# A two-layer graph transformer kernel: the widest block of destination nodes is worked in two halves, and the first table pieces start four steps later

## The chip, the cores and the metric

The kernel runs on one core of a Trainium2 chip. The metric is the time on the device for one execution, in microseconds. The core's engines are TensorE (PE), VectorE (DVE), ScalarE (ACT), GpSimd (POOL) and the queue of SyncE (SP); in the profile PEld is PE's weight load.

## The reference, cut to what matters

6250 nodes with 128 values each, 100,000 edges, 16 node types, 32 edge types, 8 heads of 16 values. Two layers like this one, a last linear map, a residual and a layer norm:

```python
k, q, v = (typed_linear(x, ntype, W).reshape(n, H, HS) for W in (Wk, Wq, Wv))
kT = jnp.einsum('nhd,htdo->nhto', k, Watt)      # a K row for every node and edge type
vT = jnp.einsum('nhd,htdo->nhto', v, Wmsg)
a = jnp.einsum('ehd,ehd->eh', kT[src, :, etype], q[dst]) * pri[:, etype].T / SQRT_D
att = edge_softmax(a, dst, n)                   # over the edges of one destination
hag = segment_sum((vT[src, :, etype] * att[:, :, None]).reshape(-1, H * HS), dst)
h = silu(typed_linear(hag, ntype, Wa))
h = layernorm(h * alpha + x * (1 - alpha)) * g + b
```

## The kernel before, in words

A first part sorts the nodes by type class and degree and writes layer 0's table to DRAM: for every node and edge type one row of 256 values, K and V (the table stores of L1110). From about 607 us on the function `edges` does both layers.

**Blocks and slots.** The destination nodes stand in 49 blocks of 128, one node a partition. A block has so many slots: slot j holds the j-th edge of each node. The widths are `OWN` (25, 21, 19, 18, 17, 16, 15, 14, 13, 12, 11) for each of four type classes and `SHARED` (41, 20, 17, 15, 14) for nodes of all classes. A slot costs one gather: POOL issues an indirect DMA (L1722) that brings 128 rows of the table, one a partition, to the ring `kvr` of `SLOTS` = 50 slots in SBUF. Nodes with very many edges take lanes of further slots: of the 41 slots of the widest block the last 12 are "riders". They get no gather; an SP copy (L1715) moves a few rows from a gathered slot (27 or 28) to them. So this block has 29 gathers and 12 copies.

**The order.** Superblocks of two to four blocks are visited in the order of `ORDERS`, one string a layer; layer 0's begins 1c 3c 1a 1b +a 2a. 1c and 3c have 13 + 12 + 11 slots each, 1a has 25 + 21 + 19 + 18 = 83 (one of them a rider), 1b 17 + 16 + 15 + 14. +a is the 41-slot block and one of 20; in layer 1 it follows 1c. POOL's order is the order in which the code is written out (`manual_schedule`); the other engines' instructions are placed by a scheduler from the same code. Layer 1's first two superblocks are begun early, under layer 0.

**One block.** Its gathers go out in chunks of up to 8 slots (`bring`, L1699); a chunk starts where the ring pointer stands and is cut at the ring's end, and if fewer than `CH` = 4 slots are left when a block begins, the pointer goes to 0 (L1668). A gather into a slot waits until DVE has last read the slot. For each chunk DVE multiplies the K half by the node's query (L1738) and sums by head (L1743). `bundles_of` (L1461) gives the order of the 41-slot block: slots 0-7 first, then 21-28 with the twelve riders, whose K products wait until the copies have read slots 27 and 28, and last 8-20.

**The rest of a block.** `finished` (L1503) is a generator. It is advanced one step a slot while the next block's slots are issued (`step`, L1688): mask (L1508), maximum (L1514), difference (L1523), exponential on ACT (L1525), its sum (L1528), then for each chunk the V half times the weights (L1541) and the adding up into the accumulator `acc` of four slots (L1552), and at the end its sum (L1557). The weights stand in the PSUM pair if 256 + 8K columns (layer 0) fit in 512, else in the SBUF tile `a`. With a superblock's last block, the node work `nodes` (L1814) is spread over the coming slots: hag (L1779), typed linear maps (masks of L300, products of L317), activation, layer norm.

**Layer 1's table.** Layer 0's `nodes` ends with K and V of the new nodes (L1895, L1899). `table` (L1599) spreads the generator `pieces_of` (L1938) over the slots of the superblock two visits on. Of each block it makes two tiles: PE products (L341), four ACT copies to the tile `st` (L348; three buffers), and a scatter on POOL (L1944), which is put in the queue 5 half steps after the tile, at the start of the next chunk's gathers (`put_due`, L1717). A superblock of k blocks gets 8k + 4 steps; the first visit's generator yields `HELP` = 4 empty steps first (L1973) and gets `HELP` more in the count (L1611). `tick` (L1428) advances these generators by steps/slots a slot.

Of the kernel before, what the change touches and what calls it, by code (L numbers as in the profile page):

```python
# [9 lines left out]
F32 = mybir.dt.float32  # L10
BF16 = mybir.dt.bfloat16
I32 = mybir.dt.int32
# [6 lines left out]
P = 128  # L19
# [15 lines left out]

HOP = 4.0
# [5 lines left out]
HELP = 4  # L42
# [59 lines left out]
def kernel(  # L102
# [1039 lines left out]
    def arm(fast):  # L1142
# [110 lines left out]
        def edges():  # L1253
# [207 lines left out]
            def bundles_of(K, riding):  # L1461
# [41 lines left out]
            def finished(v, i, chunks, kvt, used, a, pair, sums, den):  # L1503

                l, (i0, k, types), part, e = visits[v]
                K = widths(v)[i]
                av = a[:, :K, :]
                nc.vector.tensor_tensor(  # L1508
                    av, av, columns(v, i)[1].unsqueeze(2)
                    .to_broadcast([P, K, H]), op=ALU.subtract if l else ALU.add)  # L1510
                yield
                m = (best[:, e, int(part == "rest"), i, :] if part else
                     ep.tile([P, H], F32, name="m"))
# [14 lines left out]
                nc.vector.tensor_reduce(den[:, i, :], w.rearrange("p k h -> p h k"),  # L1528
# [4 lines left out]
                for j in range(len(chunks) + 1):  # L1533
                    more = []
                    if j < len(chunks):
# [4 lines left out]
                        for k0, k1 in parts:  # L1540
# [4 lines left out]
                                w[:lanes, j0 + k0:j0 + k1, :].unsqueeze(3)  # L1545
# [8 lines left out]
                    for r in used[:j]:  # L1554
                        r[2] = True
                    yield
                nc.vector.tensor_reduce(sums[:, i, :], acc.rearrange("p k c -> p c k"),  # L1557
                                        axis=AX.X, op=ALU.add)
                if i < k - 1 or part == "early":
                    return  # L1560
                if part:
# [5 lines left out]
                       + (0 if l or len(types) <= TC else 12), pace(v + 1))  # L1567

# [62 lines left out]
            for v, (l, (i0, k, types), part, e) in enumerate(visits):  # L1631
# [31 lines left out]
                for i in range(k):  # L1663
# [4 lines left out]
                    if SLOTS - room[0] < CH:  # L1668
                        room[0] = 0
                    riding = {} if part else {k: r for k, *r in tails.get(b, ((), ()))[0]}  # L1670
                    chunks, bundles, kvt, used, places = [], [], [], [], {}
                    for bundle in bundles_of(K, riding):
                        pos = room[0] + sum(k1 - k0 for k0, k1, _ in chunks)
                        cut = []
                        for k0, k1, lanes in bundle:
                            while k0 < k1:
                                size = min(k1 - k0, SLOTS - pos % SLOTS)
                                n = -(-size // (MOST if lanes == P else size))
                                cut += [(k0 + size * j // n, k0 + size * (j + 1) // n, lanes)
                                        for j in range(n)]  # L1680
                                k0, pos = k0 + size, pos + size
                        bundles += [cut] if riding and len(bundle) > 1 else [[c] for c in cut]
                        chunks += cut
                    if riding:
                        nc.vector.memset(a[:, min(riding):K], 0.0)
                    then = []

                    def step(end=False):  # L1688

                        if next(before, then) is then and not then:  # L1690
                            if i + 1 < k:
                                then.append(query(v, i + 1))
                            elif v + 1 < len(visits) and (
                                    end or not asked or all(w[0] is not asked for w in work)):
                                if asked:
                                    rush(work, asked)
                                then.append(query(v + 1, 0))
# [472 lines left out]
```

## Time and profile before

| what | value |
|---|---|
| median of 3 runs | 2912.16 us (2911.28 to 2919.52) |
| the profiled execution's own time | 2916.19 us |
| its span, first to last instruction | 2914.4 us |
| mean granted PE clock | 0.661 |
| first and last gather of a slot | 606.8 and 2842.7 us |

The span is one execution. A row of the timeline gives start, length, engine, line, operation, tiles and shapes; in brackets is the idle time of that engine before it and who ended it. "issue" means that the engine waited for nothing that the profile shows.

### The profile page before, as it was taken

How to read it: one execution, taken by the hardware profiler on the slowest of the kernel's cores; microseconds unless marked ns; L12 is line 12 of the kernel's file. 1: busy time of each engine (PE TensorE's matmuls, PEld its weight loads, DVE VectorE, ACT ScalarE, POOL GpSimd, SP SyncE). 2: the span in 40 equal slices, each digit the busy share in tenths (PEclk: the TensorE clock that was granted, in tenths of full speed). 3: DMA queues.
4: the chain of work that ended last, by engine and by line, in shares of the span. 5: the costliest groups of instructions: out<-in, count | busy, mean ns of one | idle time of the engine just before them, and what ended most of it. 6: DMA issues, size and time to landing. Idle time of an engine off the chain costs nothing. (4 is left out here: it accounts for less than half of the span.)

```text
span 2914.4 us, 22102 instructions
## 1 busy us (share of the span) xinstructions
PE 1756.3 (60%) x5415; PEld 758.2 (26%) x5415; DVE 1852.8 (64%) x4231; ACT 943.1 (32%) x1723; POOL 1985.8 (68%) x2118
## 2 busy tenths in 40 slices
PE   5999888934767787888588788601533424312122
PEld 2445444411222242223133232100211212101000
DVE  8348423247877676766577655747887777666663
ACT  4776655511433423344333455201111111101000
POOL 5333665557677677777777776767777767777776
PEclk9879767655776666567577766555656566555555
DMA  7998999988668767787776799873333333333331
GB/s 214 392 393 368 376 402 404 406 257 204 224 222 286 251 221 247 249 310 283 280 285 231 272 360 344 312 217 104 105 107 104 105 95 105 106 105 105 106 105 51
DMA packets 186099, 678.23 MB, mean 233 GB/s; under 512 B 55586, under 2 KB 101328, under 8 KB 160912
## 3 DMA queue, kind: packets, MB, share of 16 engines
q0 software_dynamic: 113248, 636.05, 61.4%
q1 hardware_dynamic: 66612, 37.21, 4.9%
q10 hardware_dynamic: 6096, 3.43, 0.5%
q8 instruction: 46, 0.75, 0.1%
q14 instruction: 97, 0.79, 0.1%
HBM read 254.44 MB, written 421.89 MB: 232 GB/s over the span
## 5 line engine op out<-in xcount | busy, mean ns | idle before, releaser
L1722 POOL DMA_INDIRECT kv<-tab,ell x1454 | 1390.9, 957 | 489.4 <-issue 370.0
L348 ACT COPY st<-tb 128x512 f32<-128x512 f32 (+1 forms) x1052 | 717.9, 755 | 577.3 <-PE tb L341 305.9
L1738 DVE TENSOR_TENSOR kv<-kv,tb 128x768 f32<-128x768 f32 (+6 forms) x278 | 262.2, 946 | 502.7 <-DMA kv<-tab,ell 329.0
L317 PE MATMUL nb<-xm,weights 128*128 128x384 f32 (+2 forms) x640 | 359.9, 716 | 324.0 <-DVE xm L300 322.3
L341 PE MATMUL tb<-bdv,kvT 32*128 32x512 f32 x784 | 287.9, 935 | 113.8 <-ACT st L348 99.7
L341 PE MATMUL tb<-bdk,kvT 32*128 32x512 f32 x784 | 294.5, 932 | 59.7 <-ACT st L348 48.0
L341 PE MATMUL tb<-bdv,vT 32*128 32x512 f32 x784 | 296.8, 830 | 34.2 <-ACT st L348 30.3
L317 PEld LDWEIGHTS nb<-xm,weights 128*128 128x128 f32 x640 | 157.4, 265 | 528.9 <-DVE xm L300 362.9
L1743 DVE TENSOR_REDUCE a<-kv 128x48 f32<-128x768 f32 (+6 forms) x278 | 260.2, 939 | 0.8
L1110 POOL DMA_INDIRECT tab<-st,rows x98 | 102.1, 1042 | 202.4 <-ACT st L348 152.7
L1552 DVE TENSOR_TENSOR tb<-kv,tb 128x512 f32<-128x512 f32 (+6 forms) x412 | 227.9, 553 | 2.0
L341 PE MATMUL tb<-bdk,kT 32*128 32x512 f32 x784 | 219.9, 839 | 1.2 <-DVE st L346 0.6
L346 DVE COPY st<-tb 128x512 f32<-128x512 f32 (+1 forms) x124 | 94.1, 759 | 191.8 <-PE tb L341 107.6
L1722 POOL DMA_INDIRECT kv<-tab,ells x166 | 159.5, 961 | 67.8 <-issue 45.1
L1541 DVE TENSOR_TENSOR kv<-kv,tb 128x768 f32<-128x768 f32 (+10 forms) x258 | 192.6, 763 | 0.9
L325 PE MATMUL nb<-ident,hag 128*128 128x128 f32 x98 | 25.5, 401 | 278.0 <-DVE hag L1779 278.0
L300 DVE SCALAR_TENSOR_TENSOR xm<-ntb,nb 128x512 f32<-128x512 bf16 (+2 forms) x224 | 126.8, 593 | 47.0 <-PE nb L325 33.4
L341 PEld LDWEIGHTS tb<-bdv,vT 32*128 32x128 f32 x784 | 119.0, 232 | 132.3 <-ACT st L348 105.7
L341 PEld LDWEIGHTS tb<-bdv,kvT 32*128 32x128 f32 x784 | 80.3, 254 | 247.0 <-ACT st L348 192.6
L341 PEld LDWEIGHTS tb<-bdk,kvT 32*128 32x128 f32 x784 | 81.0, 253 | 210.3 <-ACT st L348 166.1
L1525 ACT ACTIVATE tb<-a 128x88 f32<-128x88 f32 (+15 forms) x105 | 29.2, 278 | 324.0 <-DVE a L1523 295.2
L1944 POOL DMA_INDIRECT tab<-st,row x98 | 99.9, 1020 | 45.1 <-issue 22.0
(395 smaller groups left out, 2165.7 us busy)
## 6 DMA issues: line engine op xcount, KB each, us to landing
kv<-tab,ell POOLq DMA_INDIRECT x1454
weights<-looks SPq DMA_DIRECT2D x40, 128.0 KB
hr<-xrd SPq DMA_DIRECT2D x16, 256.0 KB
kv<-tab,ells POOLq DMA_INDIRECT x166
xrd<-xr POOLq DMA_DIRECT2D x10, 256.0 KB
weights<-looks SPq DMA_DIRECT2D x40, 64.0 KB
hrd<-hs SPq DMA_DIRECT2D x8, 256.0 KB
hr<-xrd SPq DMA_DIRECT2D x10, 192.0 KB
```

The costliest lines, as they stand in the source:

```text
L300: nc.vector.scalar_tensor_tensor(xm[:, :n], ntb[:, :n], float(t), hT[:, :n], op0=ALU.is_equal, op1=ALU.mult)
L317: nc.tensor.matmul(ps[:, :n], w[:, t, :], xm[:, :n], start=(t == types[0]), stop=(t == types[-1]))
L341: nc.tensor.matmul(pt[:, b], yT[s, i * P:(i + 1) * P], bd[s, tt, :], start=True, stop=True)
L346: nc.vector.tensor_copy(to, pt)
L348: nc.scalar.copy(to, pt)
L1110: put = nc.gpsimd.indirect_dma_start(out=tabs[0].rearrange("(n t) c -> n (t c)", t=16), out_offset=bass.IndirectOffsetOnAxis(ap=rows1[:, t ...
L1541: nc.vector.tensor_tensor((v_[:, k0:k1] if j or k0 else acc[:, :k1]) .rearrange("p k (h d) -> p k h d", h=H), v_[:, k0:k1].rearrange("p k ...
L1552: nc.vector.tensor_tensor(to, v_, to, op=ALU.add)
L1722: get = nc.gpsimd.indirect_dma_start(out=to.bitcast(I32) if l else to, out_offset=None, in_=tabs[l][:], in_offset=bass.IndirectOffsetOnAxi ...
L1738: nc.vector.tensor_tensor(kk, kk, q[:lanes].unsqueeze(1).to_broadcast([lanes, c, D]), op=ALU.mult)
L1743: nc.vector.tensor_reduce(a[:lanes, j0:j1, :], kk.rearrange("p k (h d) -> p k h d", h=H), axis=AX.X, op=ALU.add)
L1944: put = nc.gpsimd.indirect_dma_start(out=tabs[1].rearrange("(n t) c -> n (t c)", t=16), out_offset=bass.IndirectOffsetOnAxis(ap=row2[:, tg ...
```

## The change

Two things. A block of more than `HIGH` = 32 slots (only the 41-slot one, once a layer) is done in two stages, and `HELP` goes from 4 to 8.

The order of the block's gathers becomes 13-20, then 21-28 with the twelve riders (the first stage, 28 slots), then 0-12 (the second stage, 13 slots). Each stage has its own chunk list, ring start and `finished`, so its own mask, maximum, exponential and sums; the second stage's slots advance the first's `finished`. Both use the same query and the same PSUM pair; the first stage's sum goes to columns 384-511 of the pair's second bank. After the second stage `joined` takes the better of the two maxima, forms two factors with an exponential on ACT, scales the two denominators and sums by them and adds them up.

```diff
-HELP = 4
+HELP = 8
+HIGH = 32
...
                 lead = MOST if W >= 2 * MOST else 0
+                first = W - 2 * MOST if K > HIGH else 0
...
+                if first:
+                    return [[(first, W - MOST, P)], shared, [(0, first, P)]]
...
-            def finished(v, i, chunks, kvt, used, a, pair, sums, den):
+            def finished(v, i, chunks, kvt, used, a, pair, sums, den, halves=None):
-                K = widths(v)[i]
-                av = a[:, :K, :]
+                s0, s1 = min(j0 for j0, _, _ in chunks), max(j1 for _, j1, _ in chunks)
+                K = s1 - s0
+                av = a[:, s0:s1, :]
...
+                half = (s0 == 0) + 0 if halves else None
+                dens, total_ = den[:, i, :], sums[:, i, :]
+                if halves:
+                    dens = halves[1][:, half]
+                    if not half:
+                        total_ = pair[:, 1, 3 * D:4 * D]
...
-                                w[:lanes, j0 + k0:j0 + k1, :].unsqueeze(3)
+                                w[:lanes, j0 - s0 + k0:j0 - s0 + k1, :].unsqueeze(3)
...
+                if halves:
+                    if not half:
+                        return
+                    yield
+                    yield from joined(l, halves, pair[:, 1, 3 * D:4 * D], total_, den[:, i, :])
...
+            def joined(l, halves, one_, other, den):
+                mm, dd, ff = halves
+                top = ep.tile([P, H], F32, name="m")
+                nc.vector.tensor_tensor(top, mm[:, 0], mm[:, 1], op=ALU.min if l else ALU.max)
+                nc.vector.tensor_tensor(ff, mm, top.unsqueeze(1).to_broadcast([P, 2, H]),
+                                        op=ALU.subtract)
+                nc.scalar.activation(ff, ff, AF.Exp, scale=-1.0 if l else 1.0)
+                yield
+                yield
+                nc.vector.tensor_tensor(dd, dd, ff, op=ALU.mult)
+                nc.vector.tensor_tensor(den, dd[:, 0], dd[:, 1], op=ALU.add)
+                for h, of in enumerate((one_, other)):
+                    of = of.rearrange("p (h d) -> p h d", h=H)
+                    nc.vector.tensor_tensor(of, of, ff[:, h].unsqueeze(2)
+                                            .to_broadcast([P, H, HS]), op=ALU.mult)
+                yield
+                nc.vector.tensor_tensor(other, other, one_, op=ALU.add)
...
+                    bundled = bundles_of(K, riding)
+                    stages = [bundled]
+                    if K > HIGH:
+                        stages = [bundled[:2], bundled[2:]]
+                        halves = [npl.tile([P, 2, H], F32, name=f"halves{h}") for h in range(3)]
...
+                    for at, stage in enumerate(stages):
+                        if SLOTS - room[0] < CH:
+                            room[0] = 0
...
+                        then = [] if at == len(stages) - 1 else [(q, pair)]
...
+                        before = finished(v, i, chunks, kvt, used, a, pair, sums, den, halves)
```

More of the change, by code (lines that the diff above doesn't have):

```diff
@@ L1527, in finished @@
                 yield
[L1528 removed]
+                nc.vector.tensor_reduce(dens, w.rearrange("p k h -> p h k"),
                                         axis=AX.X, op=ALU.add)
@@ L1667, in edges @@
                     a = ep.tile([P, max(KB), H], F32, name="a")
-                    if SLOTS - room[0] < CH:
-                        room[0] = 0
                     riding = {} if part else {k: r for k, *r in tails.get(b, ((), ()))[0]}
[L1671 to L1683, printed above, removed]
+                    places, halves = {}, None
```

145 lines of the change are left out of this document (78 added, 67 removed).

## The prediction

> **What bounds the kernel now.** I read the page first, then the groups by line, the waits of POOL, the table of windows, and last the timeline around POOL's longest waits.
>
> ```profile
> PE 1756.3 (60%) x5415; PEld 758.2 (26%) x5415; DVE 1852.8 (64%) x4231; ACT 943.1 (32%) x1723; POOL 1985.8 (68%) x2118
> ```
> ```profile
> L1722 POOL DMA_INDIRECT kv<-tab,ell x1454 | 1390.9, 957 | 489.4 <-issue 370.0 <-DMA tab<-st,rows 15.8 <-DVE t L1798 12.9
> ```
> ```profile
> L1722 POOL DMA_INDIRECT kv<-tab,ell x1454: 940/946/2562, 606.8 to 2842.7; - x182
> ```
>
> No engine is above 68%, so the page alone names no bound. The groups do: the row gathers of L1722 run on POOL from 606.8 to 2842.7 us, 957 ns each, and most of the idle time ahead of them is "issue": POOL waited for nothing. With the 0.30 us that stands ahead of nearly each one, a gather costs 1.25 us, and POOL issues the next at once. From 607 to 2843 POOL's queue sets the pace; a wait in it is time of the whole kernel unless a later wait swallows it. The waits of POOL show which waits are more than issue:
>
> ```profile
> POOL tab L1944 <- ACT st L348: 19.0, 16, 7.6
> ...
> POOL kv L1722 <- DVE t L1798: 12.9, 2, 12.6
> ...
> POOL kv L1722 <- DVE tb L1541: 9.9, 9, 6.3
> ```
>
> The last columns are total, times and longest. Three single waits matter here: 12.6 us and 6.3 us for VectorE, and 7.6 us of a table scatter for ScalarE's copies. The windows show whether the others have room:
>
> ```profile
> 607.00:1770.00 1163.00, 855.85 (x2362) 322.76 (x2362) 792.38 (x1781) 425.63 (x649) 860.09 (x891) 0.67 0.77 261
> 1913.00:2843.00 930.00, 277.95 (x641) 136.97 (x641) 659.94 (x1522) 95.37 (x270) 699.26 (x735) 0.58 0.38 108
> ```
>
> Columns after the length: PE, PEld, DVE, ACT, POOL busy, clock, DMA share, GB/s. In layer 0 DVE is idle for 371 of 1163 us, in layer 1 for 270 of 930; ACT has more. Work added to them is hidden unless POOL waits for that very instruction.
>
> **The first wait, layer 0's 41-slot block.**
>
> ```profile
> 938.92 1.22 DVE L1738 TENSOR_TENSOR kv<-kv,tb 128x1024 f32<-128x1024 f32 x1 [9.94 <-DMA kv<-kv]
> ...
> 945.41 0.97 POOL L1722 DMA_INDIRECT kv<-tab,ell  x1 [0.30 <-issue]
> 945.55 1.79 DVE L1743 TENSOR_REDUCE a<-kv 35x16 f32<-35x256 f32 x2
> 949.39 1.26 DVE L300 SCALAR_TENSOR_TENSOR xm<-ntb,nb 128x512 f32<-128x512 bf16 x2
> 950.58 0.93 DVE L1738 TENSOR_TENSOR kv<-kv,tb 128x768 f32<-128x768 f32 x1
> 952.05 0.93 DVE L1743 TENSOR_REDUCE a<-kv 128x48 f32<-128x768 f32 x1
> 953.50 0.48 DVE L1508 TENSOR_TENSOR a<-a,neg 128x328 f32<-128x328 f32 x1
> 956.78 0.95 POOL L1722 DMA_INDIRECT kv<-tab,ell  x1 [0.30 <-issue]
> 958.49 0.47 ACT L1525 ACTIVATE a<-a 128x328 f32<-128x328 f32 x1
> 958.99 0.74 DVE L1528 TENSOR_REDUCE den<-a 128x8 f32<-128x328 f32 x1 [3.70 <-ACT a L1525]
> 959.65 1.81 DVE L1541 TENSOR_TENSOR kv<-kv,a 128x512 f32<-128x512 f32 x2
> 969.38 0.69 DVE L1541 TENSOR_TENSOR tb<-kv,a 128x512 f32<-128x512 f32 x1
> 970.34 0.96 POOL L1722 DMA_INDIRECT kv<-tab,ell  x1 [12.61 <-DVE t L1798]
> ```
>
> The ring has 50 slots. Counting the blocks' widths through the order, the 41-slot block starts at ring slot 20 and the next one (20 slots) at 11. So nine gathers of the next block (first at 945.41, last at 956.78) go into free slots, and the tenth needs slot 20, the 41-slot block's first. That slot is free only after the products with V (L1541), which wait for the softmax over all 41 slots (L1508 at 953.50), which waits for the last K product. Then the first V product into the accumulator comes last, at 969.38, 9.73 us behind the first L1541. POOL stands 12.61 us, 12.31 more than issue.
>
> After the change the first stage holds slots 13 to 40. Its lead of 8 gathers, its bundle of 8 gathers and 12 row copies (L1715), and then 13 gathers stand in POOL's and SP's queues in the counts they had before, only other columns, so both queues reach the same points at the same times, and DVE's 9.94 us wait for the copies stays. But the softmax of the 28 slots no longer needs the 13: the last reduce of the copied rows ends at 947.34 (945.55 + 1.79). One 6-slot K product and its reduce stand ahead of it in the code (0.93 + 0.93): 949.2. The typed masks of L300 (1.26) move in as they do now: 950.5. For the softmax to the accumulator product I take the shortest form the rows allow: L1508, L1514, L1523, L1528 and one L1541. The groups give their means:
>
> ```profile
> L1557 DVE TENSOR_REDUCE sums<-tb 128x128 f32<-128x512 f32 x98 | 66.5, 679 | 0.5
> L1514 DVE TENSOR_REDUCE m<-a 128x8 f32<-128x200 f32 (+12 forms) x90 | 33.9, 376 | 0.3
> L1857 DVE SCALAR_TENSOR_TENSOR hs<-hs,mv,gt 128x128 f32<-128x128 f32 x98 | 31.6, 341 | 0.0
> L1523 DVE TENSOR_TENSOR a<-a,m 128x200 f32<-128x200 f32 (+12 forms) x90 | 25.9, 288 | 0.5
> L1508 DVE TENSOR_TENSOR a<-a,neg 128x200 f32<-128x200 f32 (+12 forms) x90 | 25.8, 287 | 0.1
> L1528 DVE TENSOR_REDUCE den<-tb 128x8 f32<-128x136 f32 (+12 forms) x89 | 25.3, 285 | 26.1 <-ACT tb L1525 25.9
> ...
> L1796 DVE TENSOR_TENSOR t<-rs 128x4 f32<-128x4 f32 (+2 forms) x42 | 7.0, 167 | 5.2 <-ACT rs L1793 5.2
> ```
>
> 0.287 + 0.376 + 0.288 + 0.285 and the exponential of at most 0.47 make 1.7; with one product of 0.69, 2.4 us. The slot is free at about 953. Against that, the ring rule drops two slots: 28 slots end at ring slot 48, fewer than four are left, so the second stage starts at 0 and the next block at 13, not 11. POOL wants slot 20 two gathers earlier, at 956.78 + 1.25 - 2 x 1.25 = 955.5. So nothing may be left. If the exponential waits on ACT as now (DVE stood 3.70 for it), 956.7 and 1.2 are left; if the product into the accumulator comes 9.73 us late as now, 962.7 and 7.2, and with both 10.9. I expect the late product to go: it came of weights in SBUF (kv<-kv,a), the 328 columns being too wide for the PSUM pair in layer 0, while 224 and 104 fit, so all products then touch the pair. Value taken: 2.5 left, nearer the ACT row. **Gain 9.8 (12.3 to 1.4).**
>
> **The second, layer 1's block.**
>
> ```profile
> 2334.54 1.13 DVE L1743 TENSOR_REDUCE a<-kv 8x8 f32<-8x128 f32 x2
> 2338.28 0.95 POOL L1722 DMA_INDIRECT kv<-tab,ell  x1 [0.30 <-issue]
> 2339.17 0.48 DVE L1508 TENSOR_TENSOR a<-a,neg 128x328 f32<-128x328 f32 x1
> 2344.59 0.69 DVE L1541 TENSOR_TENSOR tb<-kv,tb 128x512 f32<-128x512 f32 x1
> 2345.56 0.94 POOL L1722 DMA_INDIRECT kv<-tab,ell  x1 [6.33 <-DVE tb L1541]
> ```
>
> Here 6.03 is above issue. POOL's distance to the slot stays nine gathers (the block now starts at ring slot 31, the next at 22), wanted at 2339.5. The copied rows are reduced by 2335.7; a 6-slot chunk (1.86) and 2.4 us as above give 2339.9: 0.4 left. With the spacing of now, L1508 to the end of the product (2339.17 to 2345.28, 6.1 us), it is 2343.7 and 4.2 left. Between the two I take 2. **Gain 4.0 (5.6 to 1.8).**
>
> **The third, the first scatter of layer 1's table.**
>
> ```profile
> 737.12 1.01 ACT L348 COPY st<-tb 128x1024 f32<-128x1024 f32 x1 [0.88 <-PE tb L341]
> 737.70 0.95 POOL L1722 DMA_INDIRECT kv<-tab,ell  x1 [0.30 <-issue]
> ...
> 744.97 1.93 ACT L348 COPY st<-tb 128x1024 f32<-128x1024 f32 x2 [0.51 <-PE tb L341]
> 746.26 1.02 POOL L1944 DMA_INDIRECT tab<-st,row  x1 [7.61 <-ACT st L348]
> ```
>
> POOL stands 7.31 us above issue until the tile's fourth copy is done. HELP gives 4 more empty steps, and the pace rises with them: 36 steps over the 83 slots of 1a, not 32. The scatter falls due on step 17, not 13: 39.2 slots after the start, not 33.7. In the timeline 103 gathers stand ahead of this scatter (the last one at 737.70), that is 36 + 36 for the two superblocks before 1a, 24 for 1a's first block and 7 for a chunk of its second. From this place and those of the next five scatters the start lies 2.6 to 5.1 slots ahead of 1a, so the due point goes from slots 28.6-31.1 to 34.1-36.6, and the scatter, which goes out at the next chunk, from slot 32 to 39: seven gathers, 8.75 us, later in POOL's queue. POOL is there at 737.70 + 1.25 + 8.75 = 747.7. What the step issues moves with it: the products of L341 on PE, the copies on ACT, the scatter on POOL; the first half tile stands 7.8 slots later in the code (step 9 of the new pace against step 5 of the old). If the copies end as now, nothing is left; if they end 7.8 x 1.25 = 9.7 us later, 8.0 is left, a loss of 0.7. They began 0.88 us after PE had finished and were limited by the node chain, not by their place, so I take 2. **Gain 5.3 (7.3 to -0.7).** Later scatters move by less and do not wait now.
>
> **What is added.** Per layer: one more set of L1508, L1514, L1523, L1528 (1.24 us), one more L1557 (0.68), and the join: four small operations like L1796 (0.67) and three of 128x128 like L1857 (1.02), in all 3.6 us of DVE, twice; on ACT two exponentials, each under 0.47. The 371 and 270 idle us of DVE hide it; without that cover it costs 7.2. New waits: DVE waits for two more exponentials. Behind the joining one in DVE's queue stand the K products of the next block; nobody needs the join itself before that superblock's node work. Other edits (the loop over stages, the index shift) issue nothing.
>
> One row bears on small DVE work beside gathers:
>
> ```profile
> 942.84 0.94 POOL L1722 DMA_INDIRECT kv<-tab,ell  x1 [0.30 <-issue]
> 943.22 0.69 DVE L1779 TENSOR_TENSOR hag<-sums,rd 128x512 f32<-128x512 f32 x1
> ```
>
> A product with both inputs in SBUF lies inside a gather, and the gather takes its usual 0.94. [...]
>
> **Sum.** 9.8 + 4.0 + 5.3 = 19.1 us. The profiled execution took 2916.2 (span 2914.4 and 1.8 around it): 2897.1. It lies 4.0 above the median of the runs, 2912.2, so 2893 for the median.
>
> **Rivals.**
> *The waits mostly come back (no change).* DVE's order keeps the accumulator product last and the scatter finds its copies late: 10.9, 4.2 and 7.3 left, a gain of 1.4 + 1.8 = 3.2, 2909. For it: 3.70 and 9.73 are what DVE's and ACT's orders made of this block once. Against: elsewhere the product into the accumulator comes first (layer 1's 2344.59). 0.19.
> *Slower: the exponentials queue behind table copies.*
>
> ```profile
> 933.31 1.93 ACT L348 COPY st<-tb 128x1024 f32<-128x1024 f32 x2 [6.75 <-DMA tab<-st,row]
> ```
>
> ACT is in order, and a copy of L348 can stand 6.75 us for an earlier scatter. In layer 0 the two halves each put an exponential there; behind it stand DVE and the V products, and POOL's gathers wait for those. If both are caught and nothing is won there, the first wait grows from 12.3 to 25.8, the scatter loses 0.7 and layer 1, which has no such copies, gains 4.0: 10.2 slower, 2922. It decides once ACT adds more to that wait than the 3.3 us then won elsewhere. For it: ACT's row; against: POOL's scatters themselves hardly wait after the first. 0.07.
> *All three go, and the earlier POOL meets no new wait:* 25.2 or a little more, 2887 to 2885; part of the forecast's upper end.
>
> **The numbers.** About 0.3% (8.7 us) is what a measurement of this kernel can tell from no change. Forecast, a gain of 9 to 27: 0.74. Range: the largest sum of gains (25.2) and a little for chance gives 2885; most of the way to the no-change rival's centre gives 2908. Outside stay the slower rival and some half of the other, under 2 in 10. Faster 0.74, within 0.3% 0.19, slower 0.07.
>
> **What would show it.** Right: POOL's wait at the tenth (layer 0: eighth) gather behind the 41-slot block falls below 4 us in both layers; the first L1944 stands behind 110 gathers and waits under 4; POOL's issue count and gather mean stay; DVE's busy time grows by up to 7 us. Wrong: the same gather still waits 10 us, or a wait as long appears in the next 100 us, or the scatter waits 7 again.

## The result

| | before | after |
|---|---|---|
| median, 7 runs each on one chip | 2917.77 us (2907.72 to 2922.90) | 2895.69 us (2886.96 to 2902.41) |
| ratio, 95% interval | | 0.993 [0.991, 0.995] |
| the profiled execution's own time | 2916.19 us | 2888.40 us |
| its span | 2914.4 us | 2886.6 us |

The change saves 22 us by the medians, 0.7%. 19.1 us were forecast. The line numbers of the changed kernel are higher: the gather is L1764 (L1722 before), the scatter of layer 1's table L1986 (L1944), mask, maximum, difference, exponential and sum L1514, L1526, L1535, L1537 and L1540, the products with V L1553 (L1541), the ACT copies L350 (L348).

### The profile after

First the line of busy times, the groups of the gather and of the scatter, and the gather's own line (shortest, median and longest in ns, then the first and last start):

```profile
PE 1770.8 (61%) x5415; PEld 757.7 (26%) x5415; DVE 1858.2 (64%) x4245; ACT 944.3 (33%) x1727; POOL 1982.4 (69%) x2118
```
```profile
L1764 POOL DMA_INDIRECT kv<-tab,ell x1454 | 1388.4, 955 | 474.0 <-issue 378.9 <-DMA tab<-st,rows 15.8 <-DMA tab<-st,row 12.3
...
L1986 POOL DMA_INDIRECT tab<-st,row x98 | 100.8, 1028 | 45.5 <-issue 22.0 <-ACT st L350 18.0 <-DMA kv<-tab,ell 1.7
```
```profile
L1764 POOL DMA_INDIRECT kv<-tab,ell x1454: 940/946/1842, 597.8 to 2815.1; - x182
```

As many gathers of the same length (955 ns, 957 before), as many POOL instructions; VectorE has 14 more and 5.4 us more work. POOL's idle time ahead of the gathers is 15.4 us less (474.0 against 489.4). The waits of POOL (total, times, longest) show which went:

```profile
POOL tab L1986 <- ACT st L350: 18.0, 21, 5.6
...
POOL kv L1764 <- DVE tb L1553: 6.2, 10, 1.8
```

The entry of 12.6 us for `t` is gone, the longest one for `tb` fell from 6.3 to 1.8. The scatter's total hardly moved (19.0 to 18.0), though its first wait went: other scatters wait now. The timeline of layer 0's 41-slot block, from the end of VectorE's long wait on (before, it was the 9.94 us for the copied rows):

```profile
925.80 1.22 DVE L1780 TENSOR_TENSOR kv<-kv,tb 128x1024 f32<-128x1024 f32 x1 [11.85 <-DMA kv<-tab,ell]
...
931.71 1.79 DVE L1785 TENSOR_REDUCE a<-kv 35x16 f32<-35x256 f32 x2
...
933.43 0.93 DVE L1780 TENSOR_TENSOR kv<-kv,tb 128x768 f32<-128x768 f32 x1
934.29 0.37 DVE L1514 TENSOR_TENSOR a<-a,neg 128x224 f32<-128x224 f32 x1
...
935.45 0.53 DVE L1526 TENSOR_REDUCE halves<-a 128x8 f32<-128x224 f32 x1
...
936.51 0.37 DVE L1535 TENSOR_TENSOR a<-a,halves 128x224 f32<-128x224 f32 x1
...
936.92 0.36 ACT L1537 ACTIVATE tb<-a 128x224 f32<-128x224 f32 x1 [7.57 <-DVE a L1535]
...
937.79 1.29 DVE L302 SCALAR_TENSOR_TENSOR xm<-ntb,nb 128x512 f32<-128x512 bf16 x2 [0.91 <-PE nb L327]
...
938.99 0.39 DVE L1540 TENSOR_REDUCE halves<-tb 128x8 f32<-128x224 f32 x1
...
939.89 0.69 DVE L1553 TENSOR_TENSOR tb<-kv,tb 128x512 f32<-128x512 f32 x1
...
940.85 0.94 POOL L1764 DMA_INDIRECT kv<-tab,ell  x1 [1.79 <-DVE tb L1553]
```

The mask of 28 slots stands 0.86 us behind the start of the second stage's first K product (6 slots), which it no longer needs, and ahead of that product's reduce. The exponential starts 0.04 us after the difference it needs, and the product into the accumulator (`tb<-kv,tb`) is the first of the products. It ends at 940.58; POOL wanted the slot at 939.36. In layer 1:

```profile
2312.62 0.37 DVE L1514 TENSOR_TENSOR a<-a,neg 128x224 f32<-128x224 f32 x1
...
2317.07 0.69 DVE L1553 TENSOR_TENSOR tb<-kv,tb 128x512 f32<-128x512 f32 x1
...
2318.03 0.94 POOL L1764 DMA_INDIRECT kv<-tab,ell  x1 [0.90 <-DVE tb L1553]
```

And the first scatter of layer 1's table, which is now behind 110 gathers:

```profile
735.86 0.95 POOL L1764 DMA_INDIRECT kv<-tab,ell  x1 [0.30 <-issue]
...
737.74 1.02 POOL L1986 DMA_INDIRECT tab<-st,row  x1 [0.93 <-ACT st L350]
```

So the three waits went from 12.61, 6.33 and 7.61 us to 1.79, 0.90 and 0.93. The gathers are the same 1620 in the same number in both kernels, so the time between two of them can be compared directly (all starts are from the two timelines, us):

| from gather to gather | holds | before | after | difference |
|---|---|---|---|---|
| start of the profile to 1 | first part, not changed | 606.83 | 597.77 | -9.06 |
| 1 to 72 | | 90.32 | 88.92 | -1.40 |
| 72 to 111 | first scatter | 59.84 | 52.37 | -7.47 |
| 111 to 232 | | 166.26 | 166.66 | +0.40 |
| 232 to 275 | layer 0's 41-slot block | 77.98 | 66.73 | -11.25 |
| 275 to 757 | | 683.83 | 685.64 | +1.81 |
| 757 to 886 | border of the layers | 227.83 | 232.69 | +4.86 |
| 886 to 1213 | | 412.92 | 412.91 | -0.01 |
| 1213 to 1240 | layer 1's 41-slot block | 40.69 | 34.38 | -6.31 |
| 1240 to 1620 | | 476.22 | 477.00 | +0.78 |
| 1620 to the end | | 71.7 | 71.5 | -0.2 |

The table is the reading to learn: 327 and 380 gathers without a wait of note cost the same to 0.2% in both kernels, so the differences belong to the places where they stand. Three places gain 25.0 us, the layers' border gives 4.9 back. From the first gather on 18.7 us are left; the other 9.1 of this one pair of profiles lie ahead of anything that was changed. At the border it is the table's last scatters that wait more. Before, then after:

```profile
1819.90 1.01 POOL L1944 DMA_INDIRECT tab<-st,row  x1 [3.02 <-ACT st L348]
...
1844.20 1.01 POOL L1944 DMA_INDIRECT tab<-st,row  x1 [4.45 <-ACT st L348]
```
```profile
1797.81 1.01 POOL L1986 DMA_INDIRECT tab<-st,row  x1 [5.65 <-ACT st L350]
...
1821.89 1.01 POOL L1986 DMA_INDIRECT tab<-st,row  x1 [5.43 <-ACT st L350]
```

### The profile page after: what moved, and what is told of

Its sections match the earlier page's. It is cut to its first block, busy times and chain, and to the rows that moved or that the text cites. A ratio compares the mean times of both kernels' runs of the same rounds, so it can differ in the third digit from the quotient of the medians.

```text
span 2886.6 us, 22118 instructions
## 1 busy us (share of the span) xinstructions
PE 1770.8 (61%) x5415; PEld 757.7 (26%) x5415; DVE 1858.2 (64%) x4245; ACT 944.3 (33%) x1727; POOL 1982.4 (69%) x2118
## 5 line engine op out<-in xcount | busy, mean ns | idle before, releaser
L1764 POOL DMA_INDIRECT kv<-tab,ell x1454 | 1388.4, 955 | 474.0 <-issue 378.9
L350 ACT COPY st<-tb 128x512 f32<-128x512 f32 (+1 forms) x1052 | 718.4, 753 | 577.9 <-PE tb L343 333.6
L1780 DVE TENSOR_TENSOR kv<-kv,tb 128x768 f32<-128x768 f32 (+10 forms) x274 | 262.4, 960 | 452.3 <-DMA kv<-tab,ell 277.6
L319 PE MATMUL nb<-xm,weights 128*128 128x384 f32 (+2 forms) x640 | 366.3, 724 | 298.9 <-DVE xm L302 292.8
L343 PE MATMUL tb<-bdk,kvT 32*128 32x512 f32 x784 | 312.3, 944 | 50.8 <-ACT st L350 38.9
L343 PE MATMUL tb<-bdv,vT 32*128 32x512 f32 x784 | 289.3, 807 | 32.1 <-ACT st L350 26.9
L1785 DVE TENSOR_REDUCE a<-kv 128x48 f32<-128x768 f32 (+10 forms) x274 | 260.6, 954 | 1.0
L1564 DVE TENSOR_TENSOR tb<-kv,tb 128x512 f32<-128x512 f32 (+7 forms) x407 | 227.2, 558 | 1.8
L348 DVE COPY st<-tb 128x512 f32<-128x512 f32 (+1 forms) x124 | 94.2, 760 | 189.5 <-PE tb L343 113.1
L1764 POOL DMA_INDIRECT kv<-tab,ells x166 | 159.1, 959 | 66.2 <-issue 44.2
L1553 DVE TENSOR_TENSOR kv<-kv,tb 128x768 f32<-128x768 f32 (+8 forms) x266 | 197.7, 761 | 0.9
L302 DVE SCALAR_TENSOR_TENSOR xm<-ntb,nb 128x512 f32<-128x512 bf16 (+2 forms) x224 | 128.5, 596 | 53.5 <-PE nb L327 36.7
L343 PEld LDWEIGHTS tb<-bdv,vT 32*128 32x128 f32 x784 | 113.0, 226 | 131.2 <-ACT st L350 105.5
L1986 POOL DMA_INDIRECT tab<-st,row x98 | 100.8, 1028 | 45.5 <-issue 22.0
L1537 ACT ACTIVATE tb<-a 128x136 f32<-128x136 f32 (+15 forms) x108 | 30.0, 278 | 290.1 <-DVE a L1535 261.0
```

What stands on the lines that cost most here:

```text
L302: nc.vector.scalar_tensor_tensor(xm[:, :n], ntb[:, :n], float(t), hT[:, :n], op0=ALU.is_equal, op1=ALU.mult)
L319: nc.tensor.matmul(ps[:, :n], w[:, t, :], xm[:, :n], start=(t == types[0]), stop=(t == types[-1]))
L343: nc.tensor.matmul(pt[:, b], yT[s, i * P:(i + 1) * P], bd[s, tt, :], start=True, stop=True)
L348: nc.vector.tensor_copy(to, pt)
L350: nc.scalar.copy(to, pt)
L1553: nc.vector.tensor_tensor((v_[:, k0:k1] if j or k0 else acc[:, :k1]) .rearrange("p k (h d) -> p k h d", h=H), v_[:, k0:k1].rearrange("p k ...
```

## The experiments

Three theories were put against each other. **A**: POOL's queue sets the pace, each of its waits is time one to one, and the three are independent. **B**: what layer 0 saves is taken back at the layers' border. **C**: the gain is a matter of the part ahead of the first gather. Two further questions are why the accumulator's product comes first now, and whether VectorE's added work is hidden.

One thing must be known to read every number below. The twelve experiments ran on three other chips, and there the kernel before itself took 3407.24, 3407.25 and 3440.43 us (e1 to e4, e5 to e8, e9 to e12), not 2918. The page of the kernel before on the third of them, e10:

```profile
span 3442.7 us, 22102 instructions
...
PE 1825.1 (53%) x5415; PEld 767.5 (22%) x5415; DVE 1873.5 (54%) x4231; ACT 947.9 (28%) x1723; POOL 1990.5 (58%) x2118
```
```profile
L1722 POOL DMA_INDIRECT kv<-tab,ell x1454: 943/949/3377, 604.5 to 3353.0; - x182
```

The gathers and VectorE's instructions take about as long as before (a gather's median is 949 ns against 946, VectorE has 1.1% more busy time; PE has 3.9% more), and the first gather starts at 604.5, as before. But the gathers take 2748 us instead of 2236: VectorE and ScalarE stand idle for reasons that the trace doesn't name, and POOL then waits for them. These rows are from e10's waits (total, times, longest):

```profile
ACT st L348 <- remote: 307.9, 53, 14.4
...
POOL tab L1944 <- ACT st L348: 221.8, 42, 14.5
...
POOL kv L1722 <- DVE tb L1541: 137.7, 21, 13.8
```

"remote" is a signal with no recorded instruction behind it; among the 200 longest waits of the kernel before on the first chip there is no such row. So on these chips POOL's queue is not alone in setting the pace, and a gain of 22 us is to be found among some 500 us of other waits. Their runs are compared among themselves only. For the places the same stretches of gathers serve as above (e1 to e11; one profile each):

| from gather to gather | 72 to 111 | 232 to 275 | 757 to 886 | 1213 to 1240 |
|---|---|---|---|---|
| before (e10) | 93.68 | 102.89 | 265.58 | 42.77 |
| later steps alone (e1, e5) | 87.91, 88.49 | 102.63, 99.02 | 262.47, 259.03 | 42.41, 42.37 |
| halves alone (e2, e6) | 93.63, 91.97 | 81.65, 83.97 | 269.10, 267.98 | 37.92, 37.95 |
| whole change (e9) | 88.27 | 86.14 | 274.46 | 39.59 |
| whole, weights in SBUF (e8) | 88.97 | 84.69 | 267.89 | 37.93 |
| whole, 80 more products (e11) | 92.00 | 86.31 | 274.42 | 38.93 |
| whole, stop in layer 0 (e3, e7) | 91.62, 89.79 | 85.38, 86.49 | 266.36, 263.90 | 38.60, 38.58 |
| whole, stop in layer 1 (e4) | 87.52 | 84.01 | 270.60 | 58.76 |

### The later steps alone, e1 and e5

```diff
 (the kernel before)
-HELP = 4
+HELP = 8
```

> The kernel before with HELP 8 alone. Theory A (each wait in POOL's queue is time of the whole kernel, and the three waits are independent): the first table scatter waits under 2 us behind 110 gathers, the waits of 12.6 and 6.3 us behind the 41-slot blocks stay, and the time falls by 6 to 7 us, ratio 0.9975 to 0.998. Theory B (what POOL gains in layer 0 is given back where layer 1's early gathers wait for the last scatters): the scatter's wait goes too, but the last gather of layer 0's part comes earlier by only 0 to 3 us. Theory C (the change's gain is a matter of the part before the first gather): no change.

> The same kernel as e1 (the later steps alone, the 41-slot block whole), on another chip if one is given where the kernel before takes about 2915 us. Theory A (each of POOL's three waits is time, one to one): the scatter wait behind gather 103 goes (6.7 us of relative time in the changed kernel), both waits inside the 41-slot blocks stay at 12 and 6 us: 2908 to 2911, ratio 0.997 to 0.9985. Theory B (what layer 0 saves before the border is taken back there, 6 us of it): ratio 0.999 to 1.000. Theory C (the gain lies ahead of the first gather, where the changed kernel's profile was 9 us earlier): the first gather comes 5 to 9 us earlier in the profile, ratio 0.995 to 0.997. In the profile, for A and B: first scatter behind 110 gathers with a wait under 2 us, and a wait of 12 us at the tenth gather behind the layer-0 block and 6 us in layer 1.

Measured: 3412.93 against 3407.24, ratio 1.0039 [1.0013, 1.0066], and on the next chip 3417.12 against 3407.25, 1.0016 [0.9991, 1.0041]. The scatter moved behind 110 gathers as worked out, and there it waited 5.22 and 6.43 us; behind 103 it waited 9.71, 11.47 and 10.02 in e10, e2 and e6. The stretch that holds it got some 5 us shorter (93.68 to 87.91 and 88.49), and yet the time is no shorter; in e1 it is longer than before by its interval. A's ratios (0.9975 to 0.998 and 0.997 to 0.9985) lie outside both intervals, B's (0.999 to 1.000) inside e5's alone. The waits at the 41-slot blocks stayed (23.21 and 19.88 us in layer 0, 7.97 and 7.96 in layer 1), so these steps have nothing to do with them. The 5 us are lost elsewhere; no stretch shows where beyond the scatter of single profiles. C falls here: the first gather came at 592.4 and 609.9 us with the same kernel on two chips, and on one chip at 592.4 to 602.5 (e1 to e4), with the part ahead of it the same in all four, so differences like the 9 us come without any change.

### The halves alone, e2 and e6

```diff
 (the changed kernel)
-HELP = 8
+HELP = 4
```

> The changed kernel with HELP back at 4: the two halves alone. Theory A: the waits behind the 41-slot blocks are 1.8 and 0.9 us as in the changed kernel, the first scatter waits 7.6 us as before, and the time falls by 14 to 16 us, ratio about 0.995. Theory B: layer 1's 5.4 us in full and of layer 0's 10.8 only some 5, in all 10 to 11. Theory C: no change.

> The same kernel as e2 (the halves alone, first superblock's pieces where they were). Theory A: both block waits go (10.8 and 5.4 us of relative time in the changed kernel), the scatter wait of 7.3 us behind gather 103 stays: 2899 to 2903 against 2917, ratio 0.994 to 0.9955. Theory B: layer 0's 10.8 us shrink to 5 at the border, layer 1's 5.4 stay: ratio 0.996 to 0.9975. Theory C: ratio 0.998 to 1.000 with the first gather where it was, or the same as the whole change if the first part moves here. In the profile, for A and B: waits under 2 us behind both 41-slot blocks, with the accumulator's product at once behind the sum of weights.

Measured: 3386.35 against 3407.24, 0.9950 [0.9921, 0.9978]; and 3391.94 against 3407.25, 0.9941 [0.9917, 0.9966]. The waits for the blocks' slots fell to 1.79 us in layer 0 (both) and 0.89 and 0.88 in layer 1, the scatter still waited 11.47 and 10.02. The two stretches of the 41-slot blocks are 19 to 21 and 5 us shorter than e10's. The places are those of theory A, and the time is shorter by 21 and 15 us. B's 10 to 11 us lie in e2's interval and at the edge of e6's, so the times alone do not exclude it.

That the times meet A's 14 to 16 us is in part luck, since these were worked out from the first chip's waits. Here the two waits were longer: against e1 and e5, on the same two chips, POOL lost 28.5 and 25.2 us of waits at the blocks, and not all of it became time. The border took 6.6 and 9.0 us more. In layer 1 a wait stands at gather 1265 that no profile with the whole block has (before, e1, e5, e10, e12); in e2:

```profile
2790.69 0.95 POOL L1764 DMA_INDIRECT kv<-tab,ell  x1 [8.23 <-DVE tb L1553]
```

The wait at gather 1302 fell from 18.0 and 18.2 to 10.2 and 10.1 in turn, so that from gather 1213 to 1334 some 4 us of the 7 are left (174.09 and 174.05 against 178.14 and 177.88). On the first chip neither kernel has a wait as long there. So one to one is not shown on these chips.

### The whole change and the kernel before, e9 and e10

> The whole change on a chip like those of e1 to e8, where the kernel before takes 3407 us and every engine but POOL shows long waits with no instruction behind them. Theory A (POOL's queue sets the pace, so that each wait taken from it is time): e6's halves gave 15 us (0.9941) and the later scatter should give 3 to 6 on top: ratio 0.992 to 0.994. Rival (on these chips VectorE and ScalarE set much of the pace, and the later scatter, which alone measured 1.0016 and 1.0039 in e5 and e1, gives nothing): ratio 0.994 to 0.998, no better than the halves alone.

> The kernel before, for a profile on such a chip beside which e1, e2, e5, e6 and e8 can be read. If the chip only adds waits and leaves the order of the work as it was, the first table scatter stands behind gather 103 and waits 10 to 12 us as in e2 and e6, the gather behind the 41-slot block (the tenth of the next block) waits 20 to 23 us in layer 0 and 8 us in layer 1 as in e1 and e5, and the first gather starts at 595 to 610 us.

e9 measured 3418.00 against 3440.43, 0.9949 [0.9923, 0.9975], which is what the halves alone gave. The interval takes in some of A's 0.992 to 0.994, but with e1 and e5 the rival is the better account: on these chips the later steps give nothing that can be measured. e10 shows the order of before, at the gathers expected: the scatter behind 103 with 9.71 us, and the two waits for the 41-slot blocks at 23.19 and 8.34 us. Layer 0's in e10:

```profile
1061.24 0.50 DVE L1523 TENSOR_TENSOR a<-a,m 128x328 f32<-128x328 f32 x1
...
1066.38 1.01 ACT L348 COPY st<-tb 128x1024 f32<-128x1024 f32 x1 [10.88 <-PE tb L341]
...
1068.88 0.47 ACT L1525 ACTIVATE a<-a 128x328 f32<-128x328 f32 x1
...
1069.38 0.75 DVE L1528 TENSOR_REDUCE den<-a 128x8 f32<-128x328 f32 x1 [7.64 <-ACT a L1525]
...
1070.04 1.82 DVE L1541 TENSOR_TENSOR kv<-kv,a 128x512 f32<-128x512 f32 x2
...
1079.69 0.16 DVE L1796 TENSOR_TENSOR t<-rs 128x4 f32<-128x4 f32 x1 [1.63 <-ACT rs L1793]
1079.77 0.69 DVE L1541 TENSOR_TENSOR tb<-kv,a 128x512 f32<-128x512 f32 x1
```
```profile
1080.73 0.95 POOL L1722 DMA_INDIRECT kv<-tab,ell  x1 [23.19 <-DVE t L1798]
```

The exponential's input is ready at 1061.74, but ScalarE stands idle for a table copy's products until 1066.38 and starts the exponential at 1068.88: it did not take the ready one first. The product into the accumulator comes 9.73 us behind the first L1541, to the hundredth what it was on the first chip. That is its place in VectorE's program: 8.1 us of it are other work of VectorE, and 1.63 us (1.64 on the first chip) a wait for ACT of the operation ahead of it.

### POOL stopped on purpose, e3, e7 and e4

```diff
 (the changed kernel, in the loop over the visits; e4: v == 24)
+                if v == 6:
+                    stop = npl.tile([P, D], F32, name="stop")
+                    for _ in range(80):
+                        nc.gpsimd.memset(stop, 0.0)
```

> The changed kernel with 80 more memsets of 128x128 on POOL at the start of the seventh superblock of layer 0: POOL issues no gather for some 15 to 17 us there. Theory A: the time grows by just that length, 15 to 17 us. Theory B: POOL comes later to the layers' border, where it waits anyway for scatters; 6 to 10 us of the stop are swallowed there and the time grows by 6 to 10 us.

> The changed kernel with 80 fills of 128x128 on POOL in the middle of layer 0 (20.9 us of POOL's queue by e3's profile: 80 fills of 0.204 us with 4.6 us between them). Theory A (POOL's queue sets the pace everywhere): 2895.7 + 21 = 2916 to 2917, ratio against the kernel before 1.000. Theory B (the layers' border takes what layer 0 saves or loses, up to the 6 us seen there): 2908 to 2911, ratio 0.997 to 0.998, and the waits of POOL between gathers 757 and 886 are 4 to 7 us shorter than in the changed kernel.

> The same stop of 80 memsets on POOL, in layer 1, at the superblock behind the 41-slot one. Theories A and B: nothing behind it waits for anything but POOL's own gathers, so the time grows by the length of the stop, 15 to 17 us. A theory by which VectorE or the node work sets layer 1's pace would have less than half of it.

The group of the stop in e3:

```profile
L1671 POOL MEMSET stop<- 128x128 f32 x80 | 16.4, 204 | 4.6
```

21 us of POOL. e3: 3412.94, 1.0026 [0.9996, 1.0056]; e7: 3416.88, 1.0024 [0.9994, 1.0055]; e4: 3422.10, 1.0045 [1.0016, 1.0074]. Against e9's 0.9949 that is 0.0077, 0.0075 and 0.0096, or 26, 26 and 33 us, with an interval of about 13 to each side. The times favour A (21) over B in layer 0 (13 to 15), but don't exclude B.

The stretches say more. In layer 0 the stop stands behind gather 347, ahead of a scatter for which POOL waits 5 to 6 us without the stop and 0.6 with it. From gather 347 to 448 POOL took 194.65 and 196.01 us, and 171.67 to 183.38 (mean 179.0) in the six profiles with the halves and no stop in layer 0: 16 of the 21 us. In layer 1 the stop is seen whole in its stretch (58.76 against 37.9 to 39.6), but the wait at gather 1265 is then gone, and from 1213 to 1334 POOL took 191.40 us against 174.05 to 177.03: 14 to 17 of the 21. So in both places a loss comes through except for what the next waits take up.

The border's stretch speaks for a part of B. On each chip it is longer with the halves: 269.10 against 262.47 (e2, e1), 267.98 against 259.03 (e6, e5), 274.46 against 265.58 (e9, e10). It goes with the time at which POOL gets there: e12, further down, has no halves but is at gather 757 40 us ahead of e10, and took 277.22; e3 and e7, 7 to 10 and 41 us behind the other profiles with the halves on their chips, took 266.36 and 263.90. Profiles that arrive together still differ by up to 5 us (e5 and e7). Who comes earlier to the border waits there longer, then, and the 4.9 us of the first chip fit this. How much of a stop comes through in layer 0 as a whole stays open to some 10 us.

### The weights in SBUF, e8

```diff
 (the changed kernel)
-                         if (2 * D + K * H) <= SB * P else av)
+                         if (2 * D + K * H) <= SB * P and not halves else av)
```

> The changed kernel, but in layer 0's 41-slot block both halves keep their weights in SBUF's a instead of PSUM beside the sums. The prediction's working (the accumulator's product comes late because the weights lie in a, and the join of the blocks waits behind it): in layer 0 POOL's wait behind the block comes back to 6 to 10 us at the eighth to tenth gather, layer 1 stays under 2. The rival (the product is early because the first half's chain of maximum, exponentials and sums is shorter and the halves are given out in another order, wherever the weights lie): the layer-0 wait stays under 3 us. Either way the time of one run moves by at most 10 us, which one run does not settle: the waits tell them apart.

One time, 3383.94. The rows of layer 0's first half:

```profile
1043.06 0.39 ACT L1537 ACTIVATE a<-a 128x224 f32<-128x224 f32 x1 [7.23 <-DVE a L1535]
...
1045.13 0.55 DVE L1540 TENSOR_REDUCE halves<-a 128x8 f32<-128x224 f32 x1
1045.60 0.69 DVE L1553 TENSOR_TENSOR tb<-kv,a 128x512 f32<-128x512 f32 x1
...
1046.56 1.14 POOL L1764 DMA_INDIRECT kv<-tab,ell  x1 [1.35 <-DVE tb L1553]
```

The weights lie in `a` (`kv,a`), and the product into the accumulator is still the first; POOL waits 1.35 us. So with the halves the product is early wherever the weights lie, as the rival had it, and the prediction's reason does not carry its forecast. VectorE's program is put in order when the kernel is built, and it is this order that places the product. With 41 slots and the weights in `a` it comes 9.73 us behind the first L1541, but with a ring of 46 (e12), the weights in `a` as well, only 3.26:

```profile
1054.12 1.29 DVE L1541 TENSOR_TENSOR kv<-kv,a 128x512 f32<-128x512 f32 x2
...
1057.38 0.70 DVE L1541 TENSOR_TENSOR tb<-kv,a 128x512 f32<-128x512 f32 x1
```

With 41 slots and the weights in PSUM (layer 1, 2344.59 in the prediction's rows) it is first. No run has layer 0's whole block with its weights in PSUM, so a share of their place there is not excluded. Why the order comes out so was not looked into further.

### More work in the join, e11

```diff
 (the changed kernel, in joined)
+                for _ in range(40):
+                    nc.vector.tensor_tensor(junk, other.rearrange("p (h d) -> p h d", h=H),
+                                            ff[:, 1].unsqueeze(2).to_broadcast([P, H, HS]),
+                                            op=ALU.mult)
```

> The changed kernel with 40 more products of 128x128 on VectorE in each of the two joins (0.34 us each by the row of the same size, 13.6 us per layer, 27 us in all; their results are not used). The prediction's step (what the change adds to VectorE lies beside POOL's queue and is hidden): the ratio stays within 0.3% of e9's. Rival (VectorE's time comes through): 27 us, 0.8% above e9's.

The 80 products stand in the trace, and cost VectorE 23.0 us:

```profile
L1603 DVE TENSOR_TENSOR junk<-sums,halves 128x128 f32<-128x128 f32 x80 | 23.0, 287 | 6.7 <-remote 5.0 <-DVE st L1976 0.3 <-DVE m L1526 0.3
```

3423.92 against the 3440.43 of the same chip, 0.9956 [0.9929, 0.9983]: 0.07% above e9. 23 us are 0.67%, and the two ratios together are known to 0.38%, so the 23 us do not come through whole; up to some 15 of them still could. The stretches tell the layers apart. In layer 0 the gathers around the products (280 to 302) took 35.27 us, and 35.13 in e9: 11.5 us are hidden, three times the change's own 3.6. In layer 1 they are not wholly hidden on this chip. At gather 1265, where the other profiles with the halves, but for e4, wait 8.2 to 9.2 us, POOL waits for the products themselves:

```profile
2805.09 0.95 POOL L1769 DMA_INDIRECT kv<-tab,ell  x1 [10.71 <-DVE junk L1603]
```

From gather 1213 to 1334 it took 181.97 us, against 174.05 to 177.03 in the six other profiles with the halves and no stop in layer 1, so 5 to 8 of the 11.5 us show there.

### A ring of 46, e12

```diff
 (the kernel before)
-SLOTS = 50
+SLOTS = 46
```

> The kernel before with a ring of 46 slots in place of 50. By the count of slots, the block behind the 41-slot one then starts 5 slots ahead of it in both layers, not 9, so that POOL wants the 41-slot block's first slot 4 gathers (5.0 us) earlier. The prediction's step (the wait is for that slot and ends when the block's first product is done, whatever POOL did before): the wait moves to the sixth gather behind the block and is 5 us longer than e10's in both layers, in layer 1 13 us against 8. Rival (the wait is for a transfer or an engine's queue that has nothing to do with the ring): it stays at the same gather and as long as it was.

The place is right, the size only in part. The wait moved from the tenth gather behind the block to the sixth in both layers, which no transfer or queue unrelated to the ring would do. In layer 0:

```profile
1041.93 1.02 POOL L1944 DMA_INDIRECT tab<-st,row  x1 [11.52 <-ACT st L348]
...
1058.35 0.98 POOL L1722 DMA_INDIRECT kv<-tab,ell  x1 [15.41 <-DVE hs L1861]
```

But it was 15.41 us in layer 0, with 11.52 already spent at a scatter ahead of it, and 6.18 in layer 1, not 28 and 13. In layer 0 the two waits follow each other at once, 26.9 us together, which is near the 28; but the place of the product in VectorE's order differs too, so this settles nothing. The smaller ring cuts the chunks elsewhere and gives VectorE another order: in layer 1 the slot was free 5 gathers and 6.18 us behind the block (12.4 us) instead of 9 gathers and 8.34 (19.6 us). So POOL wanted the slot 4 gathers earlier, as worked out, and got it 7 us earlier, which was not. The one time, 3399.63, lies below all 23 runs of the kernel before on that chip (3413.25 to 3468.14). A smaller ring that is faster is not explained, and one run is not enough to build on.

## Why the prediction was right, and where it was not

**What bounds the kernel: right on the chip it was made for.** Three waits of POOL were named, and in their three stretches 25.0 us went while 707 other gathers kept their time to 0.8 us, in one profile of each kernel.

**Layer 0's block: right, a little low.** 9.8 us were taken; the wait lost 12.61 - 1.79 = 10.8, the stretch 11.25. The next block's eighth gather waits, as counted from the dropped ring slots. 2.5 us were to be left, 1.49 above issue are: POOL came for the slot at 939.36. That so little is left is in part luck. From the mask's start to the product's end it took 6.3 us, not the 2.4 of the shortest form. VectorE did not wait for the exponential, the upper of the prediction's two values, but did other work in between: the reduce of the 6-slot product, a product of the node work (L1821) and typed masks of L302. In the prediction these stand ahead of the mask, so the mask came earlier: counted from the end of VectorE's long wait, it started after 8.5 us, not 11.6. POOL in turn wanted the slot after 13.6 us, not 16.6: the long wait did not stay at 9.94 us for a copy, it was 11.85 for a gather, and POOL's queue was further on at its end. The two shifts of 3 us cancel.

**The reason for the late product: wrong.** "it came of weights in SBUF" is the step that failed: e8 has them there and the product is early, and in e12 the whole block has them there and the product is 6.5 us earlier than before. The forecast was right for another reason, which is in the order of VectorE's program. Had the build kept the product last, the same working would have left 7.2 us of the wait in place of 2.5. The order that a build gives to an engine could be weighed as a possibility (it is part of the rival with 0.19), but not derived from the weights' place.

**Layer 1's block: 4.0 forecast, 5.4 measured**, the stretch 6.3. The spacing from mask to product shrank from 6.1 us to 5.1 (2312.62 to 2317.76), and the mask itself came early enough; 0.60 above issue is left, near the lower bound of 0.4.

**The scatter: 5.3 forecast, 6.7 measured**, behind 110 gathers as worked out. That the copies follow the node chain and not their later place in the code held on this chip (0.63 us left). On the other chips ScalarE ran late (e1 5.22, e5 6.43, e9 6.75), the wait only moved, and the later steps gave no time. That this term is time is shown by the stretch of one pair of profiles on the first chip, and by no other run.

**The sum: right by two errors that cancel.** The three terms were 3.8 us too small (22.9 measured against 19.1). What was missing is the border of the layers: "a wait as long appears in the next 100 us" was looked for near the change, but the price came 850 us later, where POOL arrives earlier at scatters whose copies do not. 4.9 us there, and 6.6 to 9.0 in the profiles on the other chips. The rest of the medians' 22 us can't be put to a place, since the first chip has one profile of each kernel; by the interval the gain is 15 to 26 us. That the time itself, 2895.69, lies so near the 2893 of the forecast is in part luck: the forecast started from a median of 2912.2 from three runs, seven runs have 2917.77, and a gain 3 us larger than forecast makes up for half of the difference.

**What is added: hidden on the first chip, as far as its stretches tell.** VectorE has 5.4 us more, up to 7 forecast. The stretches behind the two joins there grew by 1.81 us in 482 gathers and 0.78 in 380. e11 shows three times as much hidden in layer 0, but not wholly in layer 1 of another chip, where POOL has a wait at that place already.

**VectorE's products beside gathers.** The product of the prediction's one row ends 0.13 us behind its gather (943.91 against 943.78), so it is not wholly inside. e11 asks this better than the prediction's one row did, since its products have both inputs in SBUF and run without a gap beside gathers:

```profile
1098.33 9.07 DVE L1603 TENSOR_TENSOR junk<-sums,halves 128x128 f32<-128x128 f32 x28
...
1100.06 0.99 POOL L1769 DMA_INDIRECT kv<-tab,ell  x1 [0.31 <-issue]
1101.36 0.99 POOL L1769 DMA_INDIRECT kv<-tab,ell  x1 [0.30 <-issue]
...
1106.57 1.00 POOL L1769 DMA_INDIRECT kv<-tab,ell  x1 [0.30 <-issue]
...
1107.87 0.95 POOL L1769 DMA_INDIRECT kv<-tab,ell  x1 [0.30 <-issue]
```

Six gathers (L1769 here) that lie wholly beside them take 0.99 to 1.04 us, and 0.94 to 0.95 in e9, where the products are missing. So there is a cost of some 0.05 us a gather, but no gather is held for the length of the products, 9.07 us in a row here. Of the join's seven operations of VectorE, two read the first stage's sum from PSUM, which e11's products do not, so no run shows their cost; for the other five an estimate from these rows is at most some 0.25 us a layer, if each meets a gather of its own.

## What to carry to other kernels

Where one engine's queue sets the pace, count its instructions and compare two kernels between the same two of them: the stretches say where time went, when busy shares and totals of waits (19.0 against 18.0 here) do not. The waits for a buffer's slot shrank here by making what frees the slot need less (12.61 to 1.79 us and 6.33 to 0.90), but take the engine's built order as unknown until it is read from the new program. And look for the price far behind the change, at the next place where the fast engine meets another chain: here 4.9 us, 850 us later.

## What the runs showed of the hardware that was not expected

The same kernel takes 2918 us on one chip and 3407 to 3440 on three others, with gathers of the same length (a median of 946 ns before, 949 in e10) and 1.1% more busy time of VectorE. An example of what is added, from the halves alone (e2):

```profile
2414.45 0.18 DVE L1853 BATCH_NORM_AGGREGATE mv<-bn 128x2 f32<-128x6 f32 x1 [0.52 <-DVE mv L1853]
2414.55 0.66 DVE L1569 TENSOR_REDUCE sums<-tb 128x128 f32<-128x512 f32 x1
...
2419.35 0.30 ACT L1831 ACTIVATE rs<-mv,eps 128x4 f32<-128x4 f32 x1 [6.25 <-remote]
2419.35 0.17 DVE L1833 TENSOR_SCALAR v<-mv 128x4 f32<-128x4 f32 x1 [4.14 <-remote]
```

Both L1831 and L1833 need only `mv`, which was done at 2414.63; both start at 2419.35. The trace's own list of VectorE's signals has them at 2414.43, 2415.83, 2417.23, 2418.63 and 2419.33 there, 1.40 us apart and the last 0.70: as recorded they come in a slow row, long after their instructions. Of the 3791 instructions of VectorE that signal, 823 have their next recorded signal more than 1 us after their end in e2, and 4 of 3789 in the changed kernel on the first chip; e2's trace also holds only 2641 signals, the other 3784. Part of the late ones are records that are missing, then, and the rows above are those where the waiting engine was late too. Ahead of the first gather there is no loss (604.5 against 606.8 us). The cause stays open.
